# Moving two blocks' routing from the expert stage into attention, spreading the background work over more places, and summing the last results in halves

## The chip, the cores and the metric

One core of one Trainium2 chip runs the whole kernel. The metric is device time in microseconds (us), the median of several executions. Engines are named as the profile names them: PE (matmul), PEld (weight load), DVE (vector), ACT (scalar), POOL (GpSimd), SP (the queue that issues most DMAs).

## What is computed

One transformer layer on `x` of shape 4 x 2048 x 256 (4 batches, 8192 tokens, width 256), float32. Cut to what matters:

```python
h = layernorm(x) * (1 + ca) + sa                    # modulation by batch
x = x + ga * attention(h)                           # 16 heads of 16, rotary, causal softmax
h = layernorm(x) * (1 + cb) + sb
# routing: 16 experts in 4 groups, best 2 groups, best 4 experts, weights from sigmoid scores
y = sum over a token's 4 experts of  w * ((silu(h @ w1.T) * (h @ w3.T)) @ w2.T)   # inner width 192
x = x + gb * (y + shared_expert(h))
```

## The kernel before

Tokens are cut into 16 blocks of 512 (`NB = 16`, `NQ = 4` blocks a batch). The kernel has two stages, and the order of instructions on PE, ACT, DVE and POOL is written out by the program: a main loop issues its own work and, at fixed places, pulls "pieces" from Python generators (`Background`). A `yield` ends a piece; some pieces are empty and only let time pass.

**Attention.** The main loop goes over units (a pair of blocks of one batch with one group of four heads) and in each over key tiles of 128. In every batch after the first the pair (1, 2) is done before the pair (0, 3); in the last batch that is blocks 13 and 14, then 12 and 15. Line 1201 copies out one block's result for one group, so its start times mark the units. When a block has all four groups, `finish` projects it and stores it to `x1d`, and for blocks of the first phase it queues `send` in `after`, of which up to three pieces are issued in a key step if DVE and POOL have budget. `after` is also drained at the end of attention.

**Routing a block** (`send`): normalise, transpose (L260), expert scores (L384), ranks, positions by a small matmul (L402, L408), and then 16 indirect DMAs on POOL (L453), each writing 128 token rows into the expert's region of `xs`. `find_tiles` then turns the counts of a phase into a table: which expert and which rows tile 0, 1, 2, ... of 256 rows has.

**Experts.** The loop over `m` takes two tiles (a "pair") at a time. `Phase.usual` is the number of pairs always run: 52 for the first phase (blocks 0 to 11) and 20 for the second (blocks 12 to 15), 72 in all; more pairs than that are run at the very end under a condition. Iteration `m` does `inner_a` (gate and up projections, L1361), `turn(m + 1)` (transposes, L1346), `give` of the pair before (down projection L1399 and L1410, row addresses L1426 to L1453, scaling L1460 and L1462, four indirect DMAs L1464 on POOL), the loads three pairs ahead (L1330, L1332) and `inner_b`. Between these it pulls background pieces in three places, 3, 2 and 2 pieces while `m < split` and 5, 3 and 4 after (`split` = pairs of the first phase):

* `late`, before the split: `send` of the second phase's blocks and `find_tiles` of that phase.
* `rest`, from iteration `split + 1`: `back`, which for each of the 16 blocks fetches its rows, runs the shared expert (`shared`: L1504 on PE, L1516 to L1533 on ACT and DVE, L1399 and L1410 again, L1541 on DVE, L1546 on POOL), and for blocks of the first phase also `collect` (a 2 MB load of the block's 4 x 512 expert results, L1492) and `combine` (L1553 and L1556 on DVE, L1554 and L1559 on POOL, store L1560).

After the loop, the second phase's blocks are collected and combined with nothing beside them. The DMAs of SP go out in program order, so a store that waits for POOL holds what is queued behind it. The last sums of before:

```python
for n in phases[1].blocks[:2]:
    collect(n)
for n in phases[1].blocks:
    for _ in combine(n):
        pass
    if n + 2 in phases[1].blocks:
        collect(n + 2)
```

Of the kernel before, what the change touches and what calls it, by code (L numbers as in the profile page):

```python
# [8 lines left out]
F32 = mybir.dt.float32  # L9
# [20 lines left out]
TC = TT // P  # L30


PHASES = (range(NB - NQ), range(NB - NQ, NB))


ROW = D + 4 + 4 + 8
# [70 lines left out]
class Phase:  # L107


    def __init__(self, blocks):  # L110
        self.blocks = blocks
        self.tokens = len(blocks) * BT

        self.region = self.tokens + TT


        self.pairs = -(-((4 * self.tokens + E * (TT - 1)) // TT) // 2)


        self.usual = -(-(4 * self.tokens + E * TT // 2) // (2 * TT))  # L120


@with_exitstack
def adaln_attention_moe(
# [17 lines left out]
    nc = tc.nc  # L142
# [27 lines left out]
        out=earlier, in_=earlier, compare_op=ALU.is_gt, fill=0.0, base=0,  # L170
# [171 lines left out]
    def send(n, xp, tp, psum, tag, apart=1):  # L342
# [87 lines left out]
        for of, to in (  # L430
# [13 lines left out]
        nc.vector.tensor_scalar_add(  # L444
            row[:, :, D + 8 :],
            four.unsqueeze(2).to_broadcast([P, 4, 8]),
            4.0 * (n - ph.blocks[0]) * BT,
        )
        yield 0, 0, 0
        for t in range(4):  # L450
# [120 lines left out]
    with ExitStack() as actx:  # L571
# [633 lines left out]
        at = 0  # L1205
# [130 lines left out]
            issued.append(d_)  # L1336
        wts_[m], xts[m] = wt, xt

    def turn(m):

        xt = xts[m].rearrange("p c t r -> p (c t) r")
        xT = tp.tile([P, 2, 2 * TT], F32, tag="xT", name="xT")
        for k in range(2):
            pt = bank("ptx")
            for t in range(2 * TC):
                nc.tensor.transpose(  # L1346
                    pt[:, t * P : (t + 1) * P], xt[:, t, k * P : (k + 1) * P], ident
                )
            if k:
                nc.vector.tensor_copy(xT[:, k, :], pt)  # L1350
            else:
                nc.scalar.copy(xT[:, k, :], pt)
        xTs[m] = xT

    def gate_up(wt, xT, cols):


        ps = bank("gu")
        for k in range(2):
            for c_ in range(2):  # L1360
                nc.tensor.matmul(  # L1361
                    ps[:, c_ * TT : (c_ + 1) * TT],
                    lhsT=wt[:, c_, k * 2 * I + cols : k * 2 * I + cols + P],
                    rhs=xT[:, k, c_ * TT : (c_ + 1) * TT],
                    start=(k == 0 and c_ == 0),
                    stop=(k == 1),
                    skip_group_check=True,
                )
        return ps
# [117 lines left out]
    def collect(n):  # L1487

        ph = phase_of[n]
        at = 4 * (n - ph.blocks[0]) * BT  # L1490
        yg = xp.tile([P, 4, 4, D], F32, tag="yg", name="yg")
        nc.sync.dma_start(  # L1492
            yg.rearrange("p t j d -> p t (j d)"),
            ph.yd[at : at + 4 * BT, :].rearrange("(t p j) d -> p t (j d)", p=P, j=4),
        )
        results[n] = yg
# [51 lines left out]
    def combine(n):  # L1548

        yg, base = results.pop(n), bases.pop(n)  # L1550
        for t in (slice(0, 2), slice(2, 4)):
            yield 0, 0, 0
            nc.vector.tensor_add(yg[:, t, :2], yg[:, t, :2], yg[:, t, 2:])  # L1553
        nc.gpsimd.tensor_tensor(yg[:, :, 0], yg[:, :, 0], yg[:, :, 1], ALU.add)  # L1554
        yield 0, 0, 0
        nc.vector.tensor_mul(  # L1556
            yg[:, :, 0], yg[:, :, 0], gbs[:, n // NQ, :].unsqueeze(1).to_broadcast([P, 4, D])
        )
        nc.gpsimd.tensor_tensor(yg[:, :, 0], yg[:, :, 0], base, ALU.add)  # L1559
        nc.sync.dma_start(  # L1560
            out[n * BT : (n + 1) * BT, :].rearrange("(t p) d -> p t d", p=P), yg[:, :, 0]
        )
# [56 lines left out]
    for n in phases[1].blocks[:2]:  # L1619
        collect(n)  # L1620
    for n in phases[1].blocks:
        for _ in combine(n):
            pass
        if n + 2 in phases[1].blocks:
            collect(n + 2)


    with tc.If(more_tiles > 0):
# [85 lines left out]
```

## Time and profile before

| | us |
|---|---|
| median of 3 runs (lowest, highest) | 3778.42 (3774.91, 3791.0) |
| the profiled execution, device time | 3781.74 |
| its span, first to last instruction | 3779.9 |
| PE busy | 3216.2 (85%) |
| DVE busy | 2536.7 (67%) |
| ACT busy | 1505.0 (40%) |
| POOL busy | 1480.9 (39%) |

Busy times are sums over the span, with stages of different limits in them: attention until about 2712 us, experts until about 3719 us, the last sums to the end. A window line gives a stretch's start and end, its length, then each engine's busy time and number of instructions, the granted PE clock, the share of the DMA engines and GB/s. A line of the waits gives who waited for whom: total us, times, longest.

### The profile page before, as it was taken

To read this page: it belongs to the slowest core of one execution; us is meant where nothing else is said; L and a number is where in the kernel's file an instruction comes from. 1 tells how busy PE (TensorE), PEld (TensorE's weight loads), DVE (VectorE), ACT (ScalarE), POOL (GpSimd) and SP (SyncE) were. 2 spreads that over 40 slices of the span, in tenths; PEclk is the share of its full clock that TensorE was granted. 3 is DMA by queue.
4 is the path that set the end of the run, shared out by engine and by line. 5 is a ranking of instruction groups with operands and counts; after the bars stand their busy time and mean duration, and the time that the engine had idled before them with its cause. 6 is when DMAs were issued, how large, how long until landed. Compare 5 with 4: busy or idle time off the path is not lost. (4 is left out here: it accounts for less than half of the span.)

```text
span 3779.9 us, 55176 instructions
## 1 busy us (share of the span) xinstructions
PE 3216.2 (85%) x19884; PEld 1664.7 (44%) x20008; DVE 2536.7 (67%) x4518; ACT 1505.0 (40%) x2140; POOL 1480.9 (39%) x2181
## 2 busy tenths in 40 slices
PE   6878888888899889888889988898798788898893
PEld 3333333333334333333333433333376677675562
DVE  5547766676767777776776777667276577567774
ACT  2344444444455444444444444455522122221120
POOL 3132333434424353334335334210145565545554
PEclk7799989989999899989998988899898899899996
DMA  6443333322233332223334222220176667687763
GB/s 202 141 152 104 111 118 119 119 93 86 77 104 117 125 123 91 77 73 104 115 123 135 75 80 70 95 104 1 59 286 232 209 222 245 206 294 260 261 219 135
DMA packets 271164, 525.81 MB, mean 139 GB/s; under 512 B 26398, under 2 KB 146206, under 8 KB 270882
## 3 DMA queue, kind: packets, MB, share of 16 engines
q1 hardware_dynamic: 244770, 448.76, 35.0%
q0 software_dynamic: 26112, 73.44, 5.1%
q8 instruction: 160, 2.62, 0.3%
q14 instruction: 122, 1.00, 0.1%
HBM read 336.47 MB, written 185.62 MB: 138 GB/s over the span
## 5 line engine op out<-in xcount | busy, mean ns | idle before, releaser
L1258 ACT ACTIVATE e<-st 128x1024 f32<-128x1024 f32 (+3 forms) x1280 | 1078.7, 895 | 1021.8 <-PE st L1250 948.4
L980 DVE TENSOR_REDUCE mparts<-ps 128x2 f32<-128x1024 f32 (+3 forms) x1152 | 1179.7, 1044 | 445.4 <-PE ps L970 399.2
L970 PE MATMUL ps<-kt,qt 64*128 64x512 f32 (+3 forms) x3328 | 612.4, 413 | 147.2 <-ACT e L1258 65.0
L1191 PE MATMUL po<-e,vg 128*32 128x512 f32 (+3 forms) x5120 | 670.1, 589 | 36.5 <-POOL e L1262 19.9
L970 PEld LDWEIGHTS ps<-kt,qt 64*128 64x128 f32 x3328 | 303.5, 203 | 739.6 <-ACT e L1258 450.0
L1262 POOL TENSOR_SCALAR_AFFINE_SELECT e<-e 128x256 f32<-128x256 f32 x512 | 204.6, 410 | 873.0 <-ACT e L1258 869.5
L1250 PE MATMUL st<-qt,kt 64*128 64x512 f32 (+3 forms) x2560 | 462.8, 442 | 0.0
L1361 PE MATMUL gu<-xT,wt 128*128 128x256 f32 x1728 | 416.1, 396 | 17.3 <-DVE xT L1350 8.6
L1464 POOL DMA_INDIRECT yd<-yt,to x288 | 281.8, 979 | 323.5 <-ACT yt L1460 154.9
L1361 PEld LDWEIGHTS gu<-xT,wt 128*128 128x128 f32 x1728 | 332.4, 197 | 97.4 <-issue 36.8
L1243 PE MATMUL st<-mt,pick 32*128 32x512 bf16 (+3 forms) x2560 | 302.3, 372 | 77.6 <-DVE mparts L980 45.8
L453 POOL DMA_INDIRECT xs<-row,rowx x256 | 248.4, 970 | 185.0 <-DVE row L444 130.9
L1003 DVE TENSOR_REDUCE mparts<-ps 128x8 f32<-128x1024 f32 x128 | 156.7, 1224 | 174.0 <-PE ps L970 159.0
L1250 PEld LDWEIGHTS st<-qt,kt 64*128 64x128 f32 x2560 | 205.9, 199 | 137.7 <-issue 126.1
L1243 PEld LDWEIGHTS <-pick 32*128 32x128 bf16 x2560 | 87.9, 91 | 297.0 <-issue 284.4
L1460 ACT ACTIVATE yt<-y,of 128x256 f32<-128x256 f32 x144 | 60.4, 470 | 389.5 <-DVE is L1440 125.2
L895 POOL TENSOR_TENSOR r<-qk,rp 128x512 f32<-128x512 f32 x112 | 144.1, 1305 | 157.3 <-DVE qk L872 153.7
L1191 PEld LDWEIGHTS po<-e,vg 128*32 128x32 f32 x5120 | 109.0, 112 | 194.0 <-issue 124.6
L1399 PE MATMUL y<-wt,ha 128*128 128x256 f32 x576 | 148.9, 401 | 17.0 <-issue 12.4
L856 POOL TENSOR_TENSOR low<-whole,high 128x512 fp32r<-128x512 f32 x56 | 71.2, 1272 | 234.3 <-ACT whole L852 234.3
L241 POOL TENSOR_TENSOR rs<-rs,mhalf 128x4 f32<-128x4 f32 x32 | 34.9, 1089 | 252.6 <-DVE rs L240 203.8
L1399 PEld LDWEIGHTS y<-wt,ha 128*128 128x128 f32 x576 | 110.3, 202 | 36.5 <-issue 18.5
(224 smaller groups left out, 3606.4 us busy)
## 6 DMA issues: line engine op xcount, KB each, us to landing
wt<-in_w_all SPq DMA_DIRECT2D x144, 640.0 KB
kt<-kd SPq DMA_DIRECT2D x124, 512.0 KB
xt<-xs SPq DMA_DIRECT2D x144, 272.0 KB
qt<-qd SPq DMA_DIRECT2D x64, 512.0 KB
yg<-yd SPq DMA_DIRECT2D x16, 2048.0 KB
vg<-vd SPq DMA_DIRECT2D x124, 168.0 KB
xb<-in_x SPq DMA_DIRECT2D x32, 512.0 KB
qd<-high SPq DMA_DIRECT2D x112, 128.0 KB
```

The costliest lines, as they stand in the source:

```text
L453: s_ = nc.gpsimd.indirect_dma_start(out=ph.xs[:, :], out_offset=bass.IndirectOffsetOnAxis(ap=rowx[:, n, t, j : j + 1], axis=0), in_=row[:, ...
L970: nc.tensor.matmul(ps[:, half, to : to + width], lhsT=qt[rows, q, t * P : (t + 1) * P], rhs=kt[rows, q, key : key + width], start=start, s ...
L980: nc.vector.tensor_reduce(to, ps[:, :, :width], AX.X, ALU.max)
L1003: nc.vector.tensor_reduce(mine[:, :, :, 0], ps.rearrange("p h (t k) -> p h t k", k=P), AX.X, ALU.max,)
L1191: nc.tensor.matmul(po[32 * j : 32 * j + 32, off:], lhsT=va[:, k_, j * (HD + 1) : j * (HD + 1) + 32], rhs=es[j // 2][:, j % 2, off:], start ...
L1243: nc.tensor.matmul(sts[q][:, h_, off:], lhsT=pick[rows, :], rhs=mt[rows, off:], start=True, stop=False,)
L1250: nc.tensor.matmul(sts[q][:, h_, off:], lhsT=kt[rows, q, k_ * P : (k_ + 1) * P], rhs=qt[rows, q, off:], start=False, stop=True,)
L1258: nc.scalar.activation(es[q][:, :, off:], sts[q][:, :, off:], AF.Exp, scale=SCALE)
L1262: nc.gpsimd.affine_select(out=es[q][:, :, off : off + P], in_=es[q][:, :, off : off + P], compare_op=ALU.is_ge, fill=0.0, base=0, pattern= ...
L1361: nc.tensor.matmul(ps[:, c_ * TT : (c_ + 1) * TT], lhsT=wt[:, c_, k * 2 * I + cols : k * 2 * I + cols + P], rhs=xT[:, k, c_ * TT : (c_ + 1 ...
L1399: nc.tensor.matmul(pss[half][:, t, :], lhsT=ha[:, at_ : at_ + P], rhs=wt[:, half, 4 * I : 4 * I + D], start=(t == 0), stop=False, skip_gro ...
L1464: s_ = nc.gpsimd.indirect_dma_start(out=ph.yd[:, :], out_offset=bass.IndirectOffsetOnAxis(ap=to[:, t : t + 1], axis=0), in_=yt[:, t, :], i ...
```

## The change

The first phase now has 14 blocks: 0 to 11, 13 and 14. The second has blocks 12 and 15. Routing of 13 and 14 and the first phase's `find_tiles` move from the expert loop to attention's last four units. The number of pairs always run becomes 60 for the first phase and, by a new rule for a phase of few tokens, 14 for the second: 74. `send`'s modulation rows are loaded anew for the expert stage (`modbs[1] = None`). The background is pulled in seven places of an iteration, one piece each, before the split (still 7 an iteration) and in six places, four pieces each, after it (24 instead of 12). The last sums take half a block at a time, into the buffers of the expert weights, with all four half loads queued first, all arithmetic on DVE and the stores on ACT's queue.

```diff
-PHASES = (range(NB - NQ), range(NB - NQ, NB))
+PHASES = ([n for n in range(NB) if n not in (NB - NQ, NB - 1)], [NB - NQ, NB - 1])
...
-        self.usual = -(-(4 * self.tokens + E * TT // 2) // (2 * TT))
+        padding = TT // 2 if self.tokens > E * TT else 3 * TT // 4
+        self.usual = -(-(4 * self.tokens + E * padding) // (2 * TT))
...
-    def turn(m):
+    def turn(m, other=lambda: None):
...
                 nc.scalar.copy(xT[:, k, :], pt)
+                other()
...
-    def inner_a(wt, xT):
-        g, u = gate_up(wt, xT, 0), gate_up(wt, xT, P)
+    def inner_a(wt, xT, other=lambda: None):
+        g = gate_up(wt, xT, 0)
+        other()
+        u = gate_up(wt, xT, P)
...
     late, rest = Background(budget), Background(budget)
+    modbs[1] = None
...
-        def other(k):
+        def other():
             if m < split:
-                late.pull((3, 2, 2)[k])
+                late.pull(1)
             else:
-                rest.pull((5, 3, 4)[k])
+                rest.pull(4)
...
         if m < end:
-            ha = inner_a(wts_[m], xTs[m])
-            other(0)
+            ha = inner_a(wts_[m], xTs[m], other)
+            other()
             if m + 1 < end:
-                turn(m + 1)
-        other(1)
+                turn(m + 1, other)
+        other()
         if held is not None:
             give(*held)
+            other()
...
-        other(2)
+        other()
+        if m < split:
+            other()
     rest.drain()
     more_tiles = nc.values_load(beyondi[0:1, 0:1], min_val=0, max_val=E)
...
+    halves = [(n, half) for n in phases[1].blocks for half in range(2)]
+    def collect_half(n, half):
+        at = 4 * (phases[1].blocks.index(n) * BT + half * HB)
+        yg = wp.tile([P, 2, 4, D], F32, tag="wt", name="yh")
+        nc.sync.dma_start(...)
+        return yg
+    ygs = {k: collect_half(*k) for k in halves[:4]}
+    for i, (n, half) in enumerate(halves):
+        yg, y = ygs.pop((n, half)), bases[n][:, 2 * half : 2 * half + 2]
+        nc.vector.tensor_add(yg[:, :, :2], yg[:, :, :2], yg[:, :, 2:])
+        nc.vector.tensor_add(yg[:, :, 0], yg[:, :, 0], yg[:, :, 1])
+        nc.vector.tensor_mul(
+            yg[:, :, 0], yg[:, :, 0], gbs[:, n // NQ, :].unsqueeze(1).to_broadcast([P, 2, D])
+        )
+        nc.vector.tensor_add(y, y, yg[:, :, 0])
+        at = n * BT + half * HB
+        nc.scalar.dma_start(out[at : at + HB, :].rearrange("(t p) d -> p t d", p=P), y)
```

Block offsets in the phase (`n - ph.blocks[0]`) become `ph.blocks.index(n)` in `send` and `collect`.

More of the change, by code (lines that the diff above doesn't have):

```diff
@@ L446, in send @@
             four.unsqueeze(2).to_broadcast([P, 4, 8]),
-            4.0 * (n - ph.blocks[0]) * BT,
+            4.0 * ph.blocks.index(n) * BT,
         )
@@ L1489, in collect @@
         ph = phase_of[n]
-        at = 4 * (n - ph.blocks[0]) * BT
+        at = 4 * ph.blocks.index(n) * BT
         yg = xp.tile([P, 4, 4, D], F32, tag="yg", name="yg")
@@ L1615, in adaln_attention_moe @@
             held = (m, ha, hb)
-        other(2)
+        other()
+        if m < split:
+            other()
     rest.drain()
     more_tiles = nc.values_load(beyondi[0:1, 0:1], min_val=0, max_val=E)
[L1619 to L1625, printed above, removed]
+    halves = [(n, half) for n in phases[1].blocks for half in range(2)]
+    def collect_half(n, half):
+        at = 4 * (phases[1].blocks.index(n) * BT + half * HB)
+        yg = wp.tile([P, 2, 4, D], F32, tag="wt", name="yh")
+        nc.sync.dma_start(
+            yg.rearrange("p t j d -> p t (j d)"),
+            phases[1].yd[at : at + 4 * HB, :].rearrange("(t p j) d -> p t (j d)", p=P, j=4),
+        )
[7 more added lines that the diff above has]
+            yg[:, :, 0], yg[:, :, 0], gbs[:, n // NQ, :].unsqueeze(1).to_broadcast([P, 2, D])
+        )
+        nc.vector.tensor_add(y, y, yg[:, :, 0])
+        at = n * BT + half * HB
+        nc.scalar.dma_start(out[at : at + HB, :].rearrange("(t p) d -> p t d", p=P), y)
+        if i + 4 < len(halves):
+            ygs[halves[i + 4]] = collect_half(*halves[i + 4])
     with tc.If(more_tiles > 0):
```

## The prediction

> **What bounds the kernel now.** I read the page's slices, then windows cut at the stages, then single stages by their chain, waits and timeline.
>
> ```profile
> core 0: us, PE busy (x) PEld busy (x) DVE busy (x) ACT busy (x) POOL busy (x), PEclk, DMA share, GB/s
> 2148.10:2474.40 326.30, 282.24 (x1933) 119.74 (x1948) 230.20 (x362) 152.70 (x195) 114.47 (x179) 0.90 0.26 88
> 2474.40:2711.60 237.20, 219.08 (x1691) 86.72 (x1700) 141.03 (x176) 141.98 (x177) 30.79 (x68) 1.00 0.11 38
> 2756.70:3288.70 532.00, 452.18 (x2225) 362.15 (x2224) 349.64 (x1005) 132.43 (x284) 303.03 (x522) 0.91 0.66 229
> 3299.00:3353.20 54.20, 54.20 (x289) 45.01 (x289) 35.76 (x109) 16.61 (x36) 25.07 (x48) 1.00 0.80 265
> 3357.00:3702.00 345.00, 306.87 (x1280) 211.16 (x1278) 245.31 (x473) 68.16 (x152) 174.31 (x179) 0.95 0.68 247
> 3702.00:3718.70 16.70, 16.37 (x82) 12.74 (x80) 13.11 (x39) 3.78 (x9) 8.85 (x14) 1.00 0.11 41
> 3727.20:3779.90 52.70, 0.00 (x0) 0.00 (x0) 16.40 (x12) 0.00 (x0) 19.61 (x8) 0.50 0.55 200
> ```
>
> In order: the last batch's first half of attention (two prologues, two sends beside it); its last four units (12 with 15) with no background; expert iterations 0 to 43 with `late`; six bare iterations; the stage with `rest`; the loop's end; the last sums. PE sets the pace nearly everywhere: 92% busy at a full clock in attention's end, all of the time in the bare iterations. POOL is almost free in attention's end (31 of 237 us), and in the last 52.7 us nothing runs but loads, sums and stores.
>
> The chain shows what a bare iteration costs, and the waits of PE in 3386 to 3706 us what the `rest` stage loses:
>
> ```profile
> 3317.03 5.38 PE gu L1361 x24
> 3322.40 0.87 PE ptx L1346 x8
> 3323.28 1.73 PE y L1399 x8
> 3325.01 1.06 PE y L1410 x8
> ```
>
> ```profile
> PE y L1399 <- DVE sha L1520: 30.9, 9, 4.6
> ```
>
> An iteration is 5.38 + 0.87 + 1.73 + 1.06 = 9.04 us of PE. With `late` it is 532.0 / 44 = 12.1. A shared block adds 12 L1504 matmuls (5.15 in the chain) + 1.73 + 1.06 = 7.94 us of PE; it then waits for DVE's `sha`.
>
> **1. Attention's end gets two sends and a `find_tiles`.** In the built order of DVE they stand from the first (12, 15) unit to the last row maxima, none after the loop, so nothing is left to drain; the table's load is queued on SP in that loop too. What is queued behind: POOL's 16 row writes stand ahead of the causal selects (L1262), for which PE's next weighing waits.
>
> ```profile
> L453 POOL DMA_INDIRECT xs<-row,rowx x64: 956/960/972, 2835.2 to 3262.9; - x64
> ```
>
> Sorting the key steps of 850 to 2700 us in the trace by the row writes in them: 850 steps with none last 1.88 us, 18 with two 3.19, 15 with three 4.11, 4 with four 5.30. The excess, 18 x 1.31 + 15 x 2.23 + 4 x 3.42 = 71 us over 145 writes, is 0.49 us a write, 7.8 a send. A least-squares fit of the same steps charges 0.46 us per us of a send's DVE work (18.0 us in the trace: 8.3) and 4.5 for its matmuls and transposes: 20.7 us, 41 for two. Bounds: PE work alone (lines 260, 384, 402, 408 take 3.7 us of PE a send) 2 x 3.7 = 7; the price in the expert stage (below, 36 a send) 72. This stretch has more free DVE and POOL than the steps of the fit, so a little under it: **+35** (7 to 72).
>
> The row on the clock is 1.00 here without background and 0.90 with it. [...] If it fell to 0.90, 10% of 237, or 24 us, would be lost; the fit holds such losses already, so I add none.
>
> **2. Expert iterations before the split.** A send is 77 pieces, and seven an iteration stay: in the built order the sends start at iterations 0, 11, 22 and 33 before, 0 and 11 after. Before, 44 x 12.1 + 8 x 9.04 = 604 us; after, 22 x 12.1 + 38 x 9.04 = 610: **+6** for eight more iterations. `late` costs (12.1 - 9.04) x 44 = 135 us, 34 to 36 a send, now paid twice, not four times. One piece at seven places, not 3, 2 and 2, should put DVE's ranks (1.2 us each) less often in front of the experts' products. The long iterations (30.0 us at 2842.7) lie in POOL's runs of row writes, and these stay. I take **-6** (-30 to +15). Together 0. The two pairs more in all (8 - 6, 18 us) are thus counted in steps 2 and 3.
>
> **3. Iterations after the split: 14, not 20.** `rest` has 218 pieces (before 212): 24 an iteration finish it in 9.1 iterations (before 17.7), and 40 us of bare iterations follow (before 16.7). PE's work in the `rest` stage is 9.1 x 9.04 + 16 x 7.94 = 209 us; before 17.7 x 9.04 + 127 = 287, and it took 345: 58 us, or 3.6 a block, over its PE work. The same ratio gives 251, the same loss a block 267. In the built order the work between a block's last L1504 and its L1399 falls at many blocks from eight gate matmuls to four (5.38 / 12 = 0.45 us each, so 1.8 us less cover); taken for half of the blocks that is about 0.9 a block more: 267 + 14 = 281. After: 281 + 40 = 321; before 345 + 16.7 = 362: **-41** (-71 at the same ratio; +23 if the stage still takes 345). Two more blocks' `collect` and `combine` move in here at nothing: 3.7 us of DVE each (L1553 and L1556), hidden under PE's 209; with DVE the bound they cost 2 x 6, POOL's add included. The new `modb` load is one more SP issue, and its first reader waits for POOL's normalising of the block anyway (estimate: nothing).
>
> Beside a POOL add, `is` (L1440), 0.17 us alone, takes 2.34; yet L1553's median is 1.22 us and its longest 3.42, so few are held. [...] If each of the 44 POOL adds of this stage held DVE for its 2.35 us, that would be 103 us of DVE, and the gain of this step would be gone.
>
> **4. The last sums.** Before:
>
> ```profile
> 3727.19 0.93 SPq L1492 DMA_DIRECT2D yg<-yd  x2
> 3735.10 2.36 DVE L1553 TENSOR_TENSOR yg<-yg 128x1024 f32<-128x1024 f32 x2 [14.60 <-DMA yg<-yd]
> ...
> 3764.41 9.42 SPq L1560 DMA_DIRECT2D out<-yg  x2
> ...
> 3771.09 2.34 POOL L1559 TENSOR_TENSOR yg<-yg,base 128x1024 f32<-128x1024 f32 x1 [1.34 <-DVE yg L1556]
> ```
>
> Four 2 MB loads, two in flight, each later one behind a store that waits for POOL. After: 4 MB in four loads, none behind a store. The first 4 MB of before,
>
> ```profile
> DMA packets 1056, 4.19 MB, mean 280 GB/s; under 512 B 32, under 2 KB 32, under 8 KB 1056
> ```
>
> (DMA queues, 3727 to 3742 us) moved in about 12 us, at 0.4 MB a us once they ran, the first 2 MB landing 7.9 us after issue; 1 MB then lands at about 7.9 - 2.5 = 5.4, the others 2.5 apart. A half is 1.22 (L1553, 128x1024) + 3 x 0.65 (the 128x512 of L1541) = 3.2 us of DVE, so DVE sets it: 5.4 + 4 x 3.2 = 18.2, and from the last sum to the end 6.5 as now (3773.4 to 3779.9). 24.7 against 52.7: **-28** (-32 to -20; a store on ACT's queue is in no row, taken as SP's).
>
> **Sum.** 35 + 0 - 41 - 28 = -34 us on the profiled 3781.7 (span 3779.9 and 1.8 around it): 3748. That execution lies 3.3 over the median, so **3744**.
>
> **Rivals.**
>
> *Slower (0.17): the blocks' own chain paces the `rest` stage.* A block needs store, load into one of two `yg` buffers, DVE and POOL in turn; in 3386 to 3706 us SP waited 117 us in 12 waits for POOL's last add before a store. DVE's demand in the new stage, 9.1 x 5.96 + 16 x 4.3 + 14 x (3.7 + 2.35 waiting for POOL) = 208 us, equals PE's 209. If a block still takes 345 / 16 = 21.6 us, step 3 is +23 and the sum 35 + 0 + 23 - 28 = +30: 3808. It decides from 314 us, 19.6 a block, where the sum is zero. Against: PE was 89% busy there, so bare matmuls, not the chain, filled most of it.
>
> *No change (0.13).* The sends cost 55 in attention and the `rest` stage takes 295: 55 + 0 - 27 - 28 = 0: 3778.
>
> *A larger gain (0.14).* Sends find cover in attention (+15), seven places save 10 us (step 2: -4), the old ratio holds (-71): -88, 3690.
>
> *The condition at the end becomes true (0.02).* `usual` now allows 3/4 of a tile of padding an expert in the short phase, half a tile in the long one. Counting the reference's choices for the given inputs, the phases need 60 and 13 pairs against 60 and 14 run, so it does not; it would add at least 16 blocks at 21.6, 345 us.
>
> **How the numbers follow.** The forecast has 0.54, own range 3715 to 3775 (steps 1 and 3 off by 20 each). 0.5% (19 us), about what a measurement of this kernel can tell, bounds "same": 3760 to 3797. Faster: 0.14 and 0.47 of the forecast: 0.61. Slower: 0.17 + 0.02 = 0.19. Same: 0.13 and the forecast's last 0.07: 0.20. The range 3696 to 3802 leaves out the far half of the larger gain, most of the slower case, and the condition.
>
> **What would show it.** Attention's last L1201 at 2747, not 2711.6 (step 1); PEclk under 1.00 there; the 60 first pairs in 610 us with bare 9.04 us iterations from the 23rd; 16 shared blocks in about 281 us with more PE waiting for `sha`; 25 us after the last load's issue. It is wrong if blocks keep 21 us each, if attention's end grows by over 60, or if the conditional part runs.

## The result and the profile after

The changed kernel is slower: 3792.47 us median (3785.32 to 3805.21, 19 runs) against 3780.33 (3762.76 to 3791.0, 19 runs) for the kernel before beside it, ratio 1.0035, interval [1.0024, 1.0047]. The forecast was 3744. Its profiled execution took 3786.52 us (span 3784.8), 6 us under its median, so the two profiles differ by 4.9 us of span and the medians by 12.

The windows of the changed kernel, cut at the same stages as those of before (its line numbers are 2 to 5 higher than those of before; start:end, length, busy time and instructions of PE, PEld, DVE, ACT, POOL, then PEclk, DMA share, GB/s):

```profile
2151.00:2483.00 332.00, 286.45 (x1950) 119.39 (x1948) 231.60 (x346) 152.82 (x195) 120.75 (x185) 0.89 0.27 92
2483.00:2777.60 294.60, 259.58 (x1760) 102.60 (x1760) 173.41 (x290) 144.97 (x183) 83.12 (x148) 0.86 0.14 48
2819.00:3097.20 278.20, 235.47 (x1162) 186.98 (x1161) 185.80 (x529) 67.91 (x149) 155.85 (x270) 0.92 0.67 233
3097.20:3422.20 325.00, 325.00 (x1728) 269.93 (x1726) 215.00 (x653) 99.80 (x216) 150.51 (x288) 1.00 0.80 267
3424.00:3716.00 292.00, 235.22 (x888) 150.81 (x887) 201.03 (x336) 46.02 (x104) 154.16 (x123) 0.92 0.70 252
3716.00:3753.60 37.60, 37.27 (x195) 30.34 (x193) 23.82 (x76) 10.51 (x23) 18.78 (x32) 1.00 0.29 102
3753.60:3784.80 31.20, 0.34 (x2) 0.00 (x0) 14.59 (x23) 0.84 (x2) 4.42 (x10) 0.53 0.51 192
```

The second line is the place to look at: attention's last four units grew from 237.2 to 294.6 us, and PEclk there fell from 1.00 to 0.86. The fourth line is 36 bare iterations, PE busy without a gap, 9.03 us each as before. Stage by stage, in us:

| stage | before | after | difference | forecast |
|---|---|---|---|---|
| attention up to the last four units | 2474.4 | 2483.0 | +8.6 | in step 1 |
| last four units | 237.2 | 294.6 | +57.4 | step 1: +35 |
| to the first scaling of results (L1460 before, L1465 after) | 45.1 | 41.4 | -3.7 | 0 |
| from there to the first shared block | 601.7 | 606.7 | +5.0 | step 2: 0 |
| shared blocks, then bare iterations to PE's end | 360.6 | 328.3 | -32.3 | step 3: -41 |
| PE's end to the end | 60.9 | 30.9 | -30.0 | step 4: -28 |
| sum | | | +5.0 | -34 |

The waits of PE in 3424 to 3716 us (who waited for whom: total, times, longest) answer to the 30.9 us of before:

```profile
PE y L1404 <- DVE sha L1525: 56.4, 14, 7.2
```

The timeline of the changed kernel while block 13's 16 row writes run (start, length, engine, line; in brackets the idle time before and what ended it), and the window of just that stretch:

```profile
2565.92 0.98 POOL L455 DMA_INDIRECT xs<-row,rowx  x1 [0.17 <-issue]
...
2567.20 0.96 POOL L455 DMA_INDIRECT xs<-row,rowx  x1 [0.22 <-issue]
...
2568.46 0.96 POOL L455 DMA_INDIRECT xs<-row,rowx  x1 [0.22 <-issue]
...
2568.73 1.51 ACT L1260 ACTIVATE e<-st 128x768 f32<-128x768 f32 x2 [1.31 <-POOL between L465]
...
2569.46 0.77 POOL L1264 TENSOR_SCALAR_AFFINE_SELECT e<-e 128x256 f32<-128x256 f32 x2
...
2569.93 2.27 PE L1193 MATMUL po<-e,vg 128*32 128x512 f32 x8 [0.77 <-issue]
```

```profile
2564.00:2588.20 24.20, 23.43 (x130) 9.77 (x128) 10.71 (x18) 10.03 (x14) 20.35 (x42) 0.51 0.56 203
```

Three row writes, 1.3 us apart, stand between two causal selects (L1264) on POOL, and the next weighing on PE (L1193) starts 0.5 us after the second of them begins. The two selects begin 4.5 us apart; in the kernel before the 78 key steps of this stretch take 3.0 us each. In these 24 us the clock is at half (0.51), ACT and DVE are busy 10 and 11 us, and PE counts as busy but gets only 130 matmuls through. The last sums now read:

```profile
3761.94 2.10 SPq L1634 DMA_DIRECT2D yh<-yd  x4
3766.88 1.23 DVE L1643 TENSOR_TENSOR yh<-yh 128x1024 f32<-128x1024 f32 x1 [11.44 <-DMA yh<-yd]
...
3770.36 10.35 ACTq L1650 DMA_DIRECT2D out<-base  x4
...
3779.60 0.69 DVE L1648 TENSOR_TENSOR base<-base,yh 128x512 f32<-128x512 f32 x1
```

First half landed 4.9 us after the first issue, each half 3.3 us of DVE without a wait between, 4.5 us to the end: 22.9 us from the first load's issue against 52.7.

### The profile page after: what moved, and what is told of

It reads as the page before. It is cut to its first block, busy times and chain, and to the rows that moved or that the text cites. A ratio compares the mean times of both kernels' runs of the same rounds, so it can differ in the third digit from the quotient of the medians.

```text
span 3784.8 us, 55634 instructions
## 1 busy us (share of the span) xinstructions
PE 3276.9 (87%) x20104; PEld 1678.4 (44%) x20104; DVE 2542.5 (67%) x4564; ACT 1507.8 (40%) x2148; POOL 1479.2 (39%) x2193
## 5 line engine op out<-in xcount | busy, mean ns | idle before, releaser
L972 PE MATMUL ps<-kt,qt 64*128 64x512 f32 (+3 forms) x3328 | 626.9, 422 | 126.4 <-ACT e L1260 62.6
L1193 PE MATMUL po<-e,vg 128*32 128x512 f32 (+3 forms) x5120 | 684.7, 600 | 40.9 <-POOL e L1264 24.4
L1264 POOL TENSOR_SCALAR_AFFINE_SELECT e<-e 128x256 f32<-128x256 f32 x512 | 204.2, 410 | 808.2 <-ACT e L1260 804.6
L1193 PEld LDWEIGHTS po<-e,vg 128*32 128x32 f32 x5120 | 110.7, 113 | 204.4 <-issue 127.8
L1465 ACT ACTIVATE yt<-y,of 128x256 f32<-128x256 f32 x148 | 62.0, 470 | 317.1 <-PE y L1415 121.6
L1404 PE MATMUL y<-wt,ha 128*128 128x256 f32 x592 | 142.6, 384 | 0.9 <-ACT yt L1465 0.9
L1376 DVE TENSOR_TENSOR hb<-hb,gu 64x256 f32<-64x256 f32 x148 | 61.2, 413 | 101.1 <-ACT hb L1375 82.4
```

Source lines behind the costliest of these rows:

```text
L972: nc.tensor.matmul(ps[:, half, to : to + width], lhsT=qt[rows, q, t * P : (t + 1) * P], rhs=kt[rows, q, key : key + width], start=start, s ...
L1193: nc.tensor.matmul(po[32 * j : 32 * j + 32, off:], lhsT=va[:, k_, j * (HD + 1) : j * (HD + 1) + 32], rhs=es[j // 2][:, j % 2, off:], start ...
L1264: nc.gpsimd.affine_select(out=es[q][:, :, off : off + P], in_=es[q][:, :, off : off + P], compare_op=ALU.is_ge, fill=0.0, base=0, pattern= ...
L1404: nc.tensor.matmul(pss[half][:, t, :], lhsT=ha[:, at_ : at_ + P], rhs=wt[:, half, 4 * I : 4 * I + D], start=(t == 0), stop=False, skip_gro ...
```

## The experiments

They ran in five later sessions: e1 to e4, e5 to e8, e9 to e12, and e15 to e18, in which the kernel before took 3715, 3710, 3707 and 3710 us, and e13 with e14, where it took 3790. The first two were on one chip, e9 to e12 on another, and e13 to e18 on a third, which thus gave both 3790 and 3710. Whole times are therefore read as ratios to the kernel before in the same session, and stages within the four faster ones. "Loss" is a stage's time over its PE work: 9.04 us an iteration, and 7.94 a shared block.

### The parts by themselves: e1, e2, e8

e1 is the kernel before with only the last sums of the change; e2 is the change with the blocks left at 12 and 4; e8 is the change itself, unaltered.

```diff
 e2
-PHASES = ([n for n in range(NB) if n not in (NB - NQ, NB - 1)], [NB - NQ, NB - 1])
+PHASES = (list(range(NB - NQ)), list(range(NB - NQ, NB)))
...
-        padding = TT // 2 if self.tokens > E * TT else 3 * TT // 4
+        padding = TT // 2
```

> The kernel before with only the last sums changed (halves, four loads queued first, DVE alone, stores on ACT's queue), now for four blocks, so eight halves. If step 4 of the prediction is right, the first half's sum starts 5 us after the first load's issue and each half costs 3.3 us of DVE: 5 + 8 x 3.3 + 5 = 36 us after the issue against 52.7, a gain of 14 to 18 us, ratio about 0.9955. If loads, not DVE, set it (each of the last four halves waits for a buffer), it is 45 to 50 us and the gain 3 to 8.

> The changed kernel with the phases and the count of pairs of before (12 and 4 blocks, 52 and 20 pairs); places, pieces and last sums stay changed. If the loss lies in the routing moved into attention, attention ends as before (last L1201-like copy near 2711), and the whole gains: last sums 15, the rest stage as dense as in the changed kernel (5.2 us a block over its PE work, not 3.6) loses about 26: net near -15 to +15, ratio 0.996 to 1.004. If instead the places and pieces were at fault, attention ends as before and the whole is clearly slower than before, ratio over 1.006.

> The changed kernel itself, so that the others can be read against it on this chip. Expected at 1.0035 of the kernel before, with 57 us more in attention's last four units.

e1: 3697.89, ratio 0.995 [0.9933, 0.9968]. PE's end to the end took 45.1 us with four blocks; the change's 30.9 are thus about 16 us from the halves and 14 from having two blocks there, not four.

e2: 3711.56, 0.9991 [0.9979, 1.0004]. The expert loop up to the split is as long as e1's (563.4 us, and 565.6 in e1; 11.25 an iteration with `late` in both): seven places are worth nothing there. After the split, stage and bare iterations take 374.1 us where e1 takes 357.1: the new pulling of `rest` costs 17.

e8: 3736.87, 1.007 [1.0044, 1.0095], by the ratios 1.2% or some 45 us over e1. What is added to e1 by routing two blocks early, by two pairs and by the new places is a loss.

### What two sends cost in attention: e3, e4, e13

e3 lets a row write of blocks 13 and 14 go only where the key step has more POOL budget left, so that in the program's order at most one stands in a key step. e4 puts only block 13 in the first phase (13 and 3 blocks). e13 issues each of the 32 row writes twice, the second into a spare table that nothing reads.

```diff
 e3
-                yield 0, 0, 1.1
+                yield 0, 0, 3.8 if n in (13, 14) else 1.1
 e4
-PHASES = ([n for n in range(NB) if n not in (NB - NQ, NB - 1)], [NB - NQ, NB - 1])
+PHASES = ([n for n in range(NB) if n not in (12, 14, 15)], [12, 14, 15])
 e13
+                if n in (13, 14):
+                    s_ = nc.gpsimd.indirect_dma_start(out=ph.xs2[:, :], ...)
```

> The changed kernel with the 32 row writes of blocks 13 and 14 issued one a key step, not up to three. Theory A (runs of row writes on POOL hold the causal selects and the PE, whose clock then halves: 2564 to 2588 us in the changed kernel are exactly the first run): attention's last four units take 260 to 275 us, not 294.6, and the whole is 20 to 35 us faster than the changed kernel, if the later table does not hold up the experts' start. Theory B (the sends' work on DVE and PE itself costs it, whatever the pace of the writes): 285 to 300 us as in the changed kernel.

> One block less is routed in attention: the first phase has 13 blocks (0 to 11 and 13), the second 12, 14 and 15; 56 and 18 pairs, 74 in all. If each send costs attention's end 28 us (half of the 57 measured), its last four units take 264 to 268 us; if the loss is one thing set off by any background (the clock, once), 285 to 295. In the expert stage a third send costs 34 us of late work, so the whole is within 10 us of the changed kernel: what attention gains, the experts lose.

> The change itself, but each of the 32 row writes of blocks 13 and 14 in attention is issued twice, the second time to a spare table that nothing reads. Theory (the GpSimd row writes are most of the price of a send there): attention's last four units and the one before grow again by about as much as the 32 writes cost now, 35 to 60 us, and the clock there falls further under 0.88; the whole about 3775 to 3800 us on a chip where the change takes 3735. Rival (the rest of a send, its VectorE and TensorE work, is the price, and the writes only add their own 1 us each on GpSimd, which is mostly free there): under 15 us.

e3: 3713.83, 1.0006 [0.9991, 1.0022]. e4: 3748.82, 1.009 [1.0068, 1.0113], dearer than the change (1.007); its profiled run lies 13 under its median, so only its stages in attention are used; its last four units take 265.8 us, where 264 to 268 were expected. e13: 3846.52 beside 3789.84, 1.0146 [1.0121, 1.017].

Last four units, windows of e8, e3 and e13 in that order:

```profile
2462.30:2744.40 282.10, 251.46 (x1749) 100.96 (x1760) 173.81 (x290) 144.93 (x182) 83.21 (x148) 0.88 0.15 50
```

```profile
2448.00:2713.90 265.90, 241.01 (x1749) 97.23 (x1760) 172.65 (x290) 144.72 (x182) 83.15 (x148) 0.93 0.16 53
```

```profile
2500.20:2839.40 339.20, 265.50 (x1749) 104.50 (x1760) 173.93 (x290) 145.24 (x182) 116.69 (x212) 0.80 0.16 55
```

The work is the same in the first two, instruction by instruction; only the order differs, and 16 us and 0.05 of the clock with it. Of the 16, PE's busy time makes 10.5 (the same matmuls at a lower clock) and its idle time 5.7; PE waits for a select 5.0 us in e8 and 0.6 in e3. By units (start to start of the copy-outs):

| us | last of 13 with 14 | first of 12 with 15 | second | third | fourth |
|---|---|---|---|---|---|
| e1, no send | 74.1 | 66.8 | 63.5 | 63.5 | 43.3 |
| e4, 13 alone | 83.9 | 83.2 | 75.8 | 63.2 | 43.6 |
| e3, both, spaced | 80.9 | 85.1 | 66.2 | 71.4 | 43.2 |
| e8, both | 81.0 | 85.1 | 80.2 | 73.5 | 43.3 |
| the change, first session | 83.5 | 83.8 | 80.4 | 87.1 | 43.3 |
| e13, writes twice | 81.7 | 84.6 | 103.7 | 107.6 | 43.3 |

Block 13's preparation (normalise, transposes, scores, ranks) lies in the first two columns, its row writes in "second", block 14's writes in "third". Spacing the writes leaves the first two columns as they were and takes 14 us out of "second"; doubling them adds 23 and 21 to "second" and "third" and nothing elsewhere. One send (e4) costs 38 us over e1 in these columns, two (e8) 52. So the price of the two has two parts: 35 us that stay when the writes are spaced (e3 over e1), and what the runs of row writes add: 16 us in e8, and in the first session 30, if the 35 hold there too. Of the 35, 25 lie in the first two columns, ahead of any of these row writes: with block 13's preparation PE's idle time there rises from 12.6 (e1) to 23.1 us (e8), its busy time from 128.3 to 142.9, and the clock falls from 0.95 to 0.86. Doubling the writes, in a session as slow as the first, cost 43 us, within the 35 to 60 expected.

In the trace of e3 the writes do not run one to a key step. POOL has no select between most of them and runs ahead of the other engines; block 13's last 13 writes follow each other at 1.26 us, from here to 2559.5:

```profile
2542.40 0.77 POOL L1264 TENSOR_SCALAR_AFFINE_SELECT e<-e 128x256 f32<-128x256 f32 x2 [1.95 <-ACT e L1260]
2543.32 0.98 POOL L455 DMA_INDIRECT xs<-row,rowx  x1 [0.16 <-issue]
```

So it is not their pitch that e3 changes but what stands behind them on POOL.

The wait is visible where the writes are doubled. Timeline of e13:

```profile
2586.36 1.51 ACT L1271 ACTIVATE e<-st 128x768 f32<-128x768 f32 x2 [0.93 <-issue]
...
2590.62 0.96 POOL L468 DMA_INDIRECT xt<-row,rowx  x1 [0.23 <-issue]
...
2591.61 0.78 POOL L1275 TENSOR_SCALAR_AFFINE_SELECT e<-e 128x256 f32<-128x256 f32 x2
2592.09 0.19 PEld L1204 LDWEIGHTS po<-e,vg 128*32 128x32 f32 x4 [5.70 <-POOL between L476]
2592.09 2.27 PE L1204 MATMUL po<-e,vg 128*32 128x512 f32 x8 [5.30 <-POOL between L476]
```

ACT's exponentials were done at 2587.9; POOL's select came at 2591.6, the last of six row writes (three, each twice) ahead of it, and PE stood for 5.3 us. The clock is at half from 2581 to 2632 and from 2711 to 2755 in e13; the first stretch begins before this stop, behind a PE gap of 2.4 us that e3 and e8 have too, and outlasts it. In e3, where the writes of block 13 run from 2530 to 2559 as well, the clock is back at full from 2537 on:

```profile
2537.00:2561.00 24.00, 21.80 (x173) 8.83 (x170) 19.00 (x26) 12.50 (x16) 16.18 (x32) 1.00 0.31 109
```

173 matmuls in 24.0 us where the change has 130 in 24.2.

Waits for selects are not all of e13's price. In its last four units PE's longest waits have no releaser that the profile shows:

```profile
PE ps L983 <- issue: 22.7, 8, 17.3
```

The 17.3 us lie in "third", where POOL meanwhile issues 13 row writes with no select between them. So of the 43 us some 20 are such stops, and e13 does not show that the writes' place ahead of the selects costs 43. Such stops belong to the slower sessions (below).

### Pacing the expert loop too: e5, e17

e5 is e3 with two empty pieces behind each row write of the expert loop (there the late blocks 12 and 15, since 13 and 14 are routed in attention). e17 is e5 once more, in another session, beside e15 (e1 once more).

```diff
                 nc.gpsimd.memset(between, 0.0)
+                for _ in range(2 if apart == 3 else 0):
+                    yield 0, 0, 0
```

> The kernel of e3_one_write with each of the 32 row writes of blocks 12 and 15, in the expert loop, followed by two empty pieces, so that 2 to 3 of them fall in an iteration and not 7. Theory A (a run of row writes costs PE its clock and its instructions wherever it stands): the late work, 66 to 70 us over bare iterations in the changed kernel, falls to 35 or less, and the whole is 25 to 40 us faster than e3. Theory B (the work itself costs it): the late work is only spread over more iterations and its sum over bare stays within 10 us.

> The version with the last sums in halves alone, once more, as the measure for the next two on the same chip: ratio to the kernel before about 0.995; its late stage loses about 25 us a send over bare iterations on a chip where the kernel before takes 3710 us, about 33 us where it takes 3780.

> The paced version of the change (two sends in attention, one row write a key step; two in the expert loop, each row write followed by two empty pieces, so two or three in an iteration). Theory: the late stage's loss a send is half that of the version with the last sums alone on the same chip, and the iterations with two or three row writes last 9.0 us as bare ones do; ratio 0.994 to 0.997. Rival (only the faster chips gain by pacing): within 4 us a send of it, ratio 1.0 or more on a chip where the kernel before takes 3780.

e5: 3692.0, 0.9955 [0.9937, 0.9972], by the ratios 19 us under e3, where 25 to 40 were expected. e15: 3697.89, 0.9961 [0.9942, 0.998]. e17: 3696.16, 0.9953 [0.9924, 0.9982]. The `late` stages, e15 (four sends, 45 iterations) and e17 (two sends, 32 iterations):

```profile
2730.80:3234.20 503.40, 443.02 (x2274) 363.23 (x2273) 355.72 (x1027) 136.41 (x291) 308.18 (x532) 0.93 0.71 247
```

```profile
2769.80:3084.90 315.10, 301.21 (x1595) 248.22 (x1594) 237.89 (x691) 94.31 (x202) 194.47 (x342) 0.98 0.80 275
```

Loss 503.4 - 45 x 9.04 = 97 us, 24 a send, against 315.1 - 32 x 9.04 = 26, 13 a send. Cutting the trace into iterations (from one scaling on ACT to the next) and counting the row writes in each: in e17 the 14 iterations with row writes, nearly all with one to three, lose 0.6 us together; in e15 the 16 with row writes lose 46, nearly all of it in four: 23.0, 20.2, 20.4 and 16.7 us, each at the end of a block's run of writes. The iterations just before them, with three to seven writes, take 9.0 to 10.0 us. What DVE waits for in e15's late stage shows where the time goes:

```profile
DVE bst L236 <- DMA row<-x1d: 36.6, 3, 13.1
```

The rows of the next block go into the one buffer (`late`, `bufs=1`) from which the row writes read. Their load is issued 1.6 us after the last write ends, and DVE, which has the next block's first instruction (L236) in its order, stands 11.6 to 13.1 us for it, with the experts' products behind. These three waits and 6.9 us for `find_tiles`' table make 43.5 of the 46 us. In e17 DVE does not wait for rows at all and 2.9 us for the table. The row writes come so late because POOL is full: each row write and each of an iteration's four result writes takes it 1.27 us, so seven row writes with four result writes take 13.9 us, four 10.1, three 8.9 (between groups of result writes in e15, e16 and e17), and an iteration has 9.04. The rest of a send costs 12.5 us either way.

### Are the sends cheaper left where they were: e11, e14, e16

e11 is e1 with the two empty pieces and 4, 3 and 3 pieces in the three places. e14 and e16 are one kernel in two sessions: e2 with one empty piece behind each write, `late` one piece at a time, eight an iteration, and `rest` two pieces in each of six places (12 an iteration, as before).

```diff
 e11
-                late.pull((3, 2, 2)[k])
+                late.pull((4, 3, 3)[k])
 e14, e16
+                for _ in range(1 if apart == 3 else 0):
+                    yield 0, 0, 0
...
-                rest.pull(4)
+                rest.pull(2)
...
         if m < split:
             other()
+            other()
```

> The kernel before with the last sums in halves, blocks 12 and 4 and its three places, all four sends in the expert loop; only new: two empty pieces behind each row write there, and 4, 3, 3 late pieces for 3, 2, 2, so that the late list still ends by iteration 42 or so. Theory (a row write costs by how close it follows the last one, wherever it stands): the late stage's loss over bare iterations falls from 99 us to about 50, the whole to 45 to 50 us under the version with the last sums alone, about 3650 us (ratio to the kernel before about 0.983); and the expert loop is then the cheaper place for all four sends. Rival (the loss comes with the sends' other work, and pacing only spreads it): within 10 us of the version with the last sums alone, ratio 0.993 to 0.997.

> Blocks 12 and 4 as in the kernel before, so all four sends in the expert loop, with the seven places and the last sums in halves; one empty piece behind each row write there, the late list pulled one piece at a time, eight an iteration, so that each row write stands alone in its place; the rest list two pieces in each of six places (12 an iteration, as before). Theory (a row write costs by how close it follows the last one, wherever it stands): four sends cost about 12.5 to 16 us each, the late stage loses 50 to 65 us over bare iterations where the version with the last sums alone loses 99, and the whole is 3650 to 3665 us, about 35 to 50 us under that version (ratio to the kernel before 0.983 to 0.987). Rival (spacing helped the two sends of 11 and 15 because less stood beside them): loss 80 or more. On the rest stage: if 24 pieces an iteration for 12 made the rest stage dearer by 17 us, this one is within 5 us of 357 (stage and bare iterations behind it together); if the six places do it, about 374.

> All four sends in the expert loop, each row write alone in its place, four in an iteration. Theory (what counts is how many row writes fall in one iteration: two or three cost nothing, four and more cost): the late stage loses as much as in the version with the last sums alone on the same chip, within 15 us; ratio 0.992 to 0.997. Rival (the earlier result was the slower chip's): the loss falls to two thirds of it, ratio 0.983 to 0.989.

e11: 3687.48, 0.9943 [0.992, 0.9966]; 45 to 50 us under e1 were expected, and it is about level with it. e14: 3772.3 beside 3789.84, 0.9954 [0.9933, 0.9975]; no gain either. e16: 3686.74, 0.9935 [0.9911, 0.9959]. Loss of the `late` stage, split by whether an iteration holds row writes, and DVE's waits for the next block's rows and for the table:

| | sends, pieces an iteration | loss | with row writes | without | DVE for rows + table |
|---|---|---|---|---|---|
| e15 | 4, 7 | 97 | 46 | 51 | 36.6 + 6.9 |
| e16 | 4, 8, writes one apart | 92 | 25 | 67 | 18.6 + 7.2 |
| e11 | 4, 10, writes two apart | 81 | 14 | 67 | 7.9 + 3.0 |
| e17 | 2, 7, writes two apart | 26 | 1 | 25 | 0 + 2.9 |

The last column follows the loss with row writes in all four: what spacing takes away is this wait. A second `row` buffer would test it; no run has one.

Four sends with spaced writes fit before the split only with more pieces an iteration, and then their other pieces cost 67 us, not 51. In the slower session (e14) the same kernel loses 146, and the iterations with row writes lose 75. There DVE waits only 1.3 us for rows, but PE stops 33 us, a matmul or a few at a time, with no releaser that the profile shows. The profile of before, from a session as slow, has the same stops in its late stage:

```profile
PE y L1410 <- issue: 14.6, 10, 2.2
```

With those of other lines they are 33 us there, 20 in the changed kernel's profile and 28 in e13, always while POOL issues indirect writes without a pause (6 to 10 in the 12 us ahead of each stop). The 16 traces of the faster sessions have none in that stage. With spaced writes the expert loop asks 13 us a send (e17) and attention's end 17.5 (half of e3's 35, most of which is block 13's). Neither place is free, and the whole does not gain: e17 and e15 are level.

### The shared blocks: e6, e7, e9, e10, e12, e18

e6 is e5, and e7 the change, with three `rest` pieces a place for four (18 an iteration). e10 is e5 with `rest` pulled in the three old places, 10, 6 and 8 pieces. e9, and e18 in another session, are e5 with six empty pieces for three in `shared` ahead of the down projection, so that more of the experts' PE work stands between a block's L1509 and its L1404. e12 is the same edit on e11, with 5, 4 and 5 `rest` pieces.

```diff
 e6, e7
-                rest.pull(4)
+                rest.pull(3)
 e10
-                rest.pull(4)
+                rest.pull((10, 6, 8)[k])
 e9, e18, e12
-        for _ in range(3):
+        for _ in range(6):
             yield 0, 0, 0
         pss = outer(wsh, ...)
```

> e5 with three pieces at each of the six places after the split instead of four, so the rest of the work lies over about 12 of the 13 last iterations and not 9. If the density of the blocks is what raised their price from 3.4 to 5.1 us over their PE work, 12 to 25 us faster than e5. If a block costs 5 us whatever is beside it, within 5 us of e5.

> The changed kernel with three pieces, not four, at each of the six places after the split, and nothing else. Density theory: 12 to 25 us faster than the changed kernel, the stage from the first shared matmul to the last scaled block about 305 us with 12 iterations in it (PE work 236), not 290 with 9 (PE work 209). Rival (fixed price a block): no difference over 5 us.

> The paced version of the change (one row write of blocks 13 and 14 a key step in attention, two empty pieces behind each row write of 11 and 15) with three more empty pieces in each block's shared generator ahead of its outer loop; the rest list then lasts about 11 iterations at the same four pieces a place. Theory (cover): between a block's last sgu and its y matmuls there is too little other TensorE work in the seven places, so TensorE waits for sha (56 us in the change's profile); six empty pieces for three give it more cover, and the rest stage's loss over its 209 us and the bare iterations falls by 15 to 35 us, the whole to 15 to 30 us under the paced version (ratio to the kernel before 0.987 to 0.991). Rival (a fixed price for each block from the work of VectorE and GpSimd itself): within 5 us of the paced version, ratio 0.994 to 0.997.

> The same paced version, but the rest list is pulled in the three places of the kernel before, 10, 6 and 8 pieces there (24 an iteration, as many as six places of four); the late list keeps its seven places. If the six places are what made the rest stage dearer by 17 us, this is 10 to 20 us faster than the paced version (ratio to the kernel before about 0.991). If the places are innocent, it is within 5 us of it, or slower, since each place gets a larger lump.

> The version before this one (four paced sends in the expert loop, three places, last sums in halves) with six empty pieces for three in each block's shared generator and 5, 4, 5 rest pieces for 5, 3, 4. Cover theory: the rest stage's loss, some 54 us with twelve blocks, falls by 10 to 25 us and the whole with it (ratio to the kernel before about 0.978). Rival (a fixed price for each block): within 5 us of the version before this one.

> The same with three more empty pieces ahead of each block's y matmuls, the fastest version so far beside the kernel before: ratio 0.989 to 0.993 again on whichever chip; if the cover was worth something, 8 to 17 us under the version before this one on the same chip.

| | whole, us | ratio to the kernel before | shared blocks and bare iterations behind, us | against |
|---|---|---|---|---|
| e5 | 3692.0 | 0.9955 [0.9937, 0.9972] | 336.4 | |
| e6, 18 an iteration | 3687.51 | 0.9945 [0.9929, 0.9962] | 328.6 | e5: -8 |
| e7, 18 an iteration | 3732.7 | 1.0063 [1.0041, 1.0085] | 331.7 | e8: -3 |
| e10, old places | 3697.53 | 0.9965 [0.9948, 0.9983] | 337.5 | e5: +1 |
| e9, cover | 3681.65 | 0.991 [0.9888, 0.9933] | 321.9 | e5: -15 |
| e18, cover | 3676.18 | 0.9907 [0.9884, 0.9929] | 321.3 | e17: -15 |
| e12, cover | 3682.79 | 0.9926 [0.9907, 0.9944] | 345.7 | e11: -10 |

(e9 and e10 ran on another chip than e5; but e17, which is e5 on a third chip, takes 336.5 in these stages to e5's 336.4. e12 and e11 ran in the same session. The texts of e9 and e14 name blocks 11 and 15; the blocks meant are 12 and 15.) Where the pieces are pulled does not matter: e10, in the old places, takes as long as e5, and e16, with 12 an iteration in the six new places, takes 354.1 us against e15's 357.5. So the 17 us of e2 go with pulling 24 pieces an iteration for 12. Going half of the way back (e6, e7) returns 3 to 8 us, less than had been expected of it. More cover returns 10 to 15, the low end of what was expected. PE's waits for `sha` in that stage, e17 and e18:

```profile
PE y L1406 <- DVE sha L1527: 55.9, 14, 7.2
```

```profile
PE y L1406 <- DVE sha L1527: 44.4, 13, 7.6
```

e9 and e18 beat both kernels, by 0.9% over the kernel before.

## Why the prediction was wrong

**Direction.** Three of the four steps held within 9 us. Step 1 did not: +35 foretold, +66 measured (57.4, and 8.6 ahead of it, where block 13's send begins). That step failed: its price of a row write, 0.49 us each wherever it stands, and nothing for the clock. It alone turns -34 into -3; step 2 (+5) and step 3 (+9) do the rest, less 4 at the change of stages and 2 in step 4.

**Step 1, the sum.** The fit was made on wrongly cut steps. Line 1258 has 1280 exponentials and as many waits on a semaphore in the records, and both were taken as starts of steps, so the "850 steps of 1.88 us" were parts of steps. Cut by the exponentials alone, the 469 steps of 850 to 2700 us last 3.88, 3.26, 3.96, 4.50 and 6.08 us with none to four row writes; the same sum of excesses then gives some 0.2 us a write, not 0.49, further off still. A price read from such steps misses what a send does to the steps without a write: in the changed kernel these, too, went from 3.0 to 3.5 us in the last stretch. And the sends met another pace there: 2.9 row writes in a key step that has any, against 2.2 earlier, probably because no prologue takes POOL's budget.

**Step 1, the choice between bounds.** The upper bound, the price of a send in the expert loop, 36 us, came nearest: measured 33. That the two agree may be chance, for the time goes to different waits: in the expert loop to PE's stops without a releaser or to DVE's wait for rows, in attention to the clock, to block 13's preparation and to the selects. "This stretch has more free DVE and POOL" was true and beside the point. POOL was busy 83 of 295 us and DVE 173; 16 us of e8's 52 came from the order on POOL's queue, writes ahead of the selects, which the prediction named and then priced at half a microsecond a write. Some 14 more of the first session lie in "third" (87.1 us to e8's 73.5), where DVE stands 10.3 us in two waits without a releaser that the profile shows. e3 takes the writes away from the selects and lands on the 35 us of the forecast; that the figure fits is chance, as its working was wrong. What makes up these 35 us beyond the clock and PE's idle time was not taken apart further.

**The clock.** The prediction weighed the clock and added none, as "the fit holds such losses already". The row is 0.86 for 1.00, and 14% of 294.6 us is 41 us of granted clock. PE's busy time grew by 40.5 us (219.1 to 259.6), at most 7 of it the sends' own matmuls by the prediction's count, and its idle time by 16.9: most of the 57 are matmuls that took longer. e3 (0.93) and e8 (0.88) go the same way; in e13 (0.80) idle time is the larger part, 55.6 of its 102 us. Whether the clock or the gaps came first was not separated. The clock that the prediction read beside background, 0.90, pointed in the right direction; the 24 us worked out from it, and not added, were too few. Of the nine stretches of half clock that touch the changed kernel's last four units, one has a PE gap of 5.6 us beside it; the other eight follow gaps of 1.1 to 2.4 us. The kernel before has no gap over 1 us there and the full clock. The longest half clock of the changed kernel there lasts 24 us, 2564 to 2588; PE's longest gap in the records is 2.4 us just before, and 0.8 within. The records have PE busy in 23.4 of those 24 us and the clock stays at half; whether the records, in which the ends of matmuls are modelled, show too much busy time there, and what brings the full clock back, the runs do not tell. The same kernel in e8 keeps the half clock for 10 us at that place.

**Step 2.** Eight more iterations at 9.04 came, +5. The 6 us for pieces one at a time did not: 12.10 us an iteration with `late`, 12.09 before; e2 against e1 shows the same.

**Step 3.** 290.2 us for the shared blocks against 281, 38.1 bare against 40. The loss a block rose from 3.6 to 5.1 us, not to 4.5. The term was of the right kind, PE waiting for `sha` (56.4 us against 30.9), but it was put down to the new places; e10 and e16 show that it is not the places, and e2, e6 and e7 that it goes with the density. With 14 iterations behind the split for 16 blocks the density is part of moving the split. How density lengthens the wait for `sha` was not tested; the trace has DVE standing 37.8 us in this stage for POOL's add (L1559), with later work queued behind. The 103 us that were weighed for DVE held by POOL's 44 adds did not come: of DVE's L1558 ten of 28 take 2.2 to 3.4 us, not the median of 1.22, and of L1445 five of nine 2.3, not 0.17: 31 us over in all, as in the kernel before (nine of 24 and six of 17, 18 and 13 us; more than the prediction's "few"). So that did not set the difference.

**Step 4.** -30 for -28: the best priced part, worked out load by load from rows of before. e1 shows that the sums in halves do not need the other parts.

**The rivals.** The blocks' own chain did not take over: 18.1 us a block, under its break-even of 19.6. "No change" had the right mechanism, dear sends and 295 us of `rest`, at 0.13. The conditional part did not run. The slower side came from a rise of step 1 that stood in the text as a bound and in none of the rivals.

**Open.** Why all kernels are some 2% slower in some sessions was not found. A part is where PE, and in attention DVE and ACT, stand during indirect writes with no releaser shown: in the late stage 33 us of the profile of before, none of e15's. That fits the dearer runs of row writes there (30 us against 16 in attention); what stops the engines, the profiles do not show.

## What to carry to other kernels

Free time on an engine priced nothing here (POOL was busy 83 of 295 us, and that stretch still grew by 57): 16 us of the two sends' price came from what their writes stood in front of in POOL's order (e8 over e3), so read which instruction waits behind it and put short DMAs where none does. Ask also what waits for its buffer: here the next block's load waited for the last write, and DVE for the load (36.6 us in three waits, e15). When the same work shows a price in another stage of the same trace, demand a reason for a lower one (36 us a send in the expert loop, 33 measured in attention). The background list pulled twice as densely lost 5.1 us a block for 3.6, so ending it earlier gained 32 us, where the ratio of before would have given 71.

## What the runs showed of the hardware that was not expected

- 16 indirect row writes on POOL, 0.96 us each at a pitch of 1.27 us, with selects between them that PE waits for, went with 24 us at half PE clock; 32 of them with 51 us (e13). The pitch alone does not do it: the same kernel in e8 had 10 us, and in e3 13 writes ran at that pitch with no select between them while the clock was full.
- The half clock came behind PE gaps of 1.1 to 2.4 us in eight of nine cases (the changed kernel's last four units).
- POOL has room for three such row writes beside four result writes in a 9 us iteration (8.9 us in e17). With seven (13.9 us, e15) PE's iterations still take 9 us at first; the loss comes at the end, where DVE waits for the load that the last write holds up (36.6 us in three waits).
- A kernel's time moved by 2% between sessions (3710 and 3790 us for the kernel before), on one chip too, with bare iterations at 9.04 us in both: the difference is in the stages with background. In the slower ones PE stops 20 to 33 us in the late stage while POOL issues indirect writes, with no releaser shown; in the faster ones it does not.
